# Two attention layers on one core: every engine's order from a list scheduler in the source, norms on ScalarE, layer 1's norm from layer 0's statistics

## Chip, cores, metric

One NeuronCore of a Trainium2 chip. The metric is device time in microseconds (us) of one execution.

## The reference, cut to what matters

Input x is 128 batches of 128 x 512 in float32, with a 128 x 128 adjacency mask for each batch. Two layers follow each other:

```python
x = layernorm(x + L0(x, adj))      # 4 heads of 64: q, k, v, masked softmax, out projection
x = layernorm(x + L1(x, adj))      # own norm first, then 8 heads of 64, mask | identity
# layernorm(x) = (x - mean) / sqrt(var + 1e-5); L1 norms its input again, with gamma and beta
```

So x1 = norm(y) leaves layer 0, and layer 1 first computes h = norm(x1). With v the variance of y, the mean of x1 is 0 and its variance is v / (v + eps). Hence h = (y - mean) / sqrt(v (1 + eps) + eps^2): both norms follow from one set of statistics of y.

## The kernel before

It works on groups of four batches (32 groups). A *unit* is eight heads' worth of attention: two batches of layer 0 or one of layer 1, so a group has 2 + 4 units. TensorE's order is written by hand; the other engines' order is the framework's. A slot starts one unit, finishes the unit two slots older, and puts *filling* (projections of other groups) between the stages in fixed shares:

```python
def slot(u, fill):
    stages = ((scores, u, 0.4), (attend, recent[1], 0.2), (residual, recent[1], 0.2),
              (probs_t, recent[0], 0.2))
    ...
        stage(unit)
        for step in fill[done:upto]:   # the share of filling after this stage
            step()
...
def residual(u):                       # the output projection, the sum and the norms
        nc.gpsimd.tensor_tensor(xb, xin, (bias0, bias1)[l], op=ALU.add)
        for c in range(nk):
            nc.tensor.matmul(pm, aT[:, j * nk + c, :], WO[l][:, c, :], ...)
        nc.vector.tensor_add(y, pm, xb)
        if l == 0:
            normed(X1[g][:, b, :], y, ...)
            normed(H[g][:, b, :], X1[g][:, b, :], ...)   # a second pass of statistics
        else:
            normed(y, y, ...)
...
def normed(dst, src, name):
    norm_stats(src, 0, mv)             # VectorE bn_stats, bn_aggr
    r = rstd_of(mv, 1)                 # GpSimd add eps, pow -0.5
    nc.vector.tensor_scalar(dst, src, mv[:, 0, 0:1], r, op0=ALU.subtract, op1=ALU.mult)
```

`attend` ends in an eviction from PSUM to the tile aT, and `residual` needs aT; only a fifth of the slot's filling lies between them. `probs_t` transposes the probabilities and evicts them to the tile pT. The eviction to aT is always ScalarE's; the others alternate between ScalarE and VectorE by the parity of an index.

Of the kernel before, what the change touches and what calls it, by code (L numbers as in the profile page):

```python
# [10 lines left out]
F32 = mybir.dt.float32  # L11
# [5 lines left out]
PE = mybir.EngineType.PE  # L17

P = 128
D = 64  # L20
# [4 lines left out]
SCALE = D ** -0.5  # L25


@with_exitstack
def kernel(ctx: ExitStack, tc: tile.TileContext, x, adj, wq, wk, wv, wo, bo,
# [9 lines left out]
    const = ctx.enter_context(tc.tile_pool(name="const", bufs=1))  # L39
    one = ctx.enter_context(tc.tile_pool(name="one", bufs=1))  # L40
    two = ctx.enter_context(tc.tile_pool(name="two", bufs=2))
    three = ctx.enter_context(tc.tile_pool(name="three", bufs=3))
    ps_sc = ctx.enter_context(tc.tile_pool(name="ps_sc", bufs=1, space=PSUM))
    ps_tr = ctx.enter_context(tc.tile_pool(name="ps_tr", bufs=2, space=PSUM))
    ps_ao = ctx.enter_context(tc.tile_pool(name="ps_ao", bufs=2, space=PSUM))
    ps_mm = ctx.enter_context(tc.tile_pool(name="ps_mm", bufs=2, space=PSUM))
    ctx.enter_context(tc.manual_schedule(engines={PE}))

    def tr_tile(name):
        return ps_tr.tile([P, 512], F32, tag="tr", name=name)  # L50

    def mm_tile(name):
        return ps_mm.tile([P, 512], F32, tag="mm", name=name)


    X, M = {}, {}

    def load(g):
        X[g] = two.tile([P, G, E], F32, tag="x", name=f"x_{g}")
        M[g] = three.tile([P, G, N], U8, tag="m", name=f"m_{g}")  # L60
        nc.sync.dma_start(X[g], x[g * G:(g + 1) * G].rearrange("b n e -> n b e"))
        nc.sync.dma_start(M[g], adj[g * G:(g + 1) * G].rearrange("b i j -> i b j"))

    load(0)


    ident = const.tile([P, P], F32, name="ident")
    make_identity(nc, ident)
    eye = const.tile([P, P], U8, name="eye")
    nc.vector.tensor_copy(eye, ident)  # L70
    mhalf = const.tile([P, G], F32, name="mhalf")
    nc.gpsimd.memset(mhalf, -0.5)

    w0 = const.tile([P, KC, 3 * INNER[0]], F32, name="w0")
    for i, w in enumerate((wq, wk, wv)):
        nc.sync.dma_start(w0[:, :, i * INNER[0]:(i + 1) * INNER[0]],
                          w.rearrange("(c p) f -> p c f", p=P))
    nc.gpsimd.tensor_scalar_mul(w0[:, :, :INNER[0]], w0[:, :, :INNER[0]], SCALE)
    wo0 = const.tile([P, INNER[0] // P, E], F32, name="wo0")
    nc.sync.dma_start(wo0, wo.rearrange("(c p) f -> p c f", p=P))  # L80
    bias0 = const.tile([P, E], F32, name="bias0")
    nc.sync.dma_start(bias0, bo[None, :].to_broadcast([P, E]))
    bias1 = const.tile([P, E], F32, name="bias1")
    nc.sync.dma_start(bias1, b_out[None, :].to_broadcast([P, E]))

    w1 = const.tile([P, KC, 3 * INNER[1]], F32, name="w1")
    wo1 = const.tile([P, INNER[1] // P, E], F32, name="wo1")
    gb_raw = const.tile([2 * KC, P], F32, name="gb_raw")
    gb = const.tile([P, 2 * KC], F32, name="gb")

    def transposed_weight(dst, src, name, r, scale):
        rows, cols = src.shape
        raw = two.tile([P, cols], F32, tag="raw", name=f"{name}_{r}")
        nc.sync.dma_start(raw, src[r * P:(r + 1) * P, :])

        def run():
            pt = tr_tile(f"{name}t_{r}")
            for c in range(cols // P):
                nc.tensor.transpose(pt[:, c * P:(c + 1) * P], raw[:, c * P:(c + 1) * P], ident)
            dst_r = dst[:, :, r * P:(r + 1) * P]  # L100
            src_r = pt.rearrange("p (c f) -> p c f", f=P)
            if r % 2:
                nc.vector.tensor_scalar_mul(dst_r, src_r, scale)
            else:
                nc.scalar.activation(dst_r, src_r, AF.Copy, scale=scale)
        return run

    def setup_layer1():

        nc.sync.dma_start(gb_raw[:KC], gamma.rearrange("(c p) -> c p", p=P))  # L110
        nc.sync.dma_start(gb_raw[KC:], beta.rearrange("(c p) -> c p", p=P))

        def gb_step():
            pt = tr_tile("gb_t")
            nc.tensor.transpose(pt[:, :2 * KC], gb_raw, ident[:2 * KC, :2 * KC])
            nc.vector.tensor_copy(gb, pt[:, :2 * KC])

        def step(dst, src, name, r, scale):
            def run():
                transposed_weight(dst, src, name, r, scale)()  # L120
            return run

        nq = INNER[1] // P
        return ([gb_step] + [step(w1, w_qkv, "w_qkv", r, SCALE if r < nq else 1.0) for r in range(3 * nq)]
                + [step(wo1, w_out, "w_out", r, 1.0) for r in range(E // P)])

    W = (w0, w1)
    WO = (wo0, wo1)
    X1, H, XT, QK, V = {}, {}, {}, {}, {}


    def transposed_steps(l, g):
        def chunk(c):
            def run():
                src = X[g] if l == 0 else H[g]
                if c == 0:
                    XT[l, g] = one.tile([P, KC, T], F32, tag=f"xT{l}", name=f"xT{l}_{g}")
                xT = XT[l, g]
                pt = tr_tile(f"xt{l}_{g}_{c}")
                for b in range(G):  # L140
                    nc.tensor.transpose(pt[:, b * N:(b + 1) * N], src[:, b, c * P:(c + 1) * P], ident)  # L141
                if l == 0:
                    if c % 2:
                        nc.vector.tensor_copy(xT[:, c, :], pt)
                    else:
                        nc.scalar.copy(xT[:, c, :], pt)
                else:
                    nc.scalar.activation(xT[:, c, :], pt, AF.Identity,
                                         bias=gb[:, KC + c:KC + c + 1], scale=gb[:, c:c + 1])
            return run  # L150
        return [chunk(c) for c in range(KC)]

    def project_steps(l, g):
        I = INNER[l]
        nq = I // P
        per = 512 // I
        steps = []
        box = {}

        def begin():  # L160
            QK[l, g] = one.tile([P, 2 * nq, T], F32, tag=f"qk{l}", name=f"qk{l}_{g}")
            V[l, g] = one.tile([P, G, I], F32, tag=f"v{l}", name=f"v{l}_{g}")

        def qk_step(f, c):
            def run():
                if f == 0 and c == 0:
                    begin()
                if c == 0:
                    box["pm"] = mm_tile(f"qk{l}_{g}_{f}")
                pm = box["pm"]  # L170
                nc.tensor.matmul(pm, W[l][:, c, f * P:(f + 1) * P], XT[l, g][:, c, :],  # L171
                                 start=(c == 0), stop=(c == KC - 1))
                if c == KC - 1:
                    if f % 2:
                        nc.scalar.copy(QK[l, g][:, f, :], pm)  # L175
                    else:
                        nc.vector.tensor_copy(QK[l, g][:, f, :], pm)  # L177
            return run

        def v_step(b0, b, cs):  # L180
            def run():
                if b == b0 and cs[0] == 0:
                    box["pm"] = mm_tile(f"v{l}_{g}_{b0}")
                pm = box["pm"]
                for c in cs:
                    nc.tensor.matmul(pm[:, (b - b0) * I:(b - b0 + 1) * I],  # L186
                                     XT[l, g][:, c, b * N:(b + 1) * N], W[l][:, c, 2 * I:3 * I],
                                     start=(c == 0), stop=(c == KC - 1))
                if b == b0 + per - 1 and cs[-1] == KC - 1:
                    src = pm.rearrange("p (b i) -> p b i", i=I)  # L190
                    if (b0 // per) % 2:
                        nc.scalar.copy(V[l, g][:, b0:b0 + per, :], src)
                    else:
                        nc.vector.tensor_copy(V[l, g][:, b0:b0 + per, :], src)
            return run

        for f in range(2 * nq):
            steps += [qk_step(f, c) for c in range(KC)]
        for b0 in range(0, G, per):
            for b in range(b0, b0 + per):  # L200
                steps += [v_step(b0, b, range(c, c + per)) for c in range(0, KC, per)]
        return steps



    SM, PT, AT = {}, {}, {}

    def batches(u):
        l, g, k = u
        per = 8 // HEADS[l]  # L210
        return range(k * per, (k + 1) * per)

# [206 lines left out]
```

## Time and profile before

| | before |
|---|---|
| median time | 4197.6 us |
| TensorE busy / idle | 3705 / 492 us |
| mean granted TensorE clock | 0.932 |
| VectorE, ScalarE, GpSimd busy | 1700, 1124, 1208 us |

"Busy" of TensorE counts pipelined matmuls at whatever clock they ran, so 88% busy does not mean 88% useful; the sum of the same work at full clock, 3320 us, is worked out in the prediction from the rows of a stretch without waits. The prediction also shows the lines of this profile. In them PE and PEld are TensorE's matmuls and its weight loads, DVE is VectorE, ACT ScalarE, POOL GpSimd and SP the engine that issues the transfers; a line of waits, "A <- B: 266.8, 128, 5.4", says that A waited for B 266.8 us in total, 128 times, at most 5.4 us.

### The profile page before, as it was taken

To read this page: it belongs to the slowest core of one execution; us is meant where nothing else is said; L and a number is where in the kernel's file an instruction comes from. 1 tells how busy PE (TensorE), PEld (TensorE's weight loads), DVE (VectorE), ACT (ScalarE), POOL (GpSimd) and SP (SyncE) were. 2 spreads that over 40 slices of the span, in tenths; PEclk is the share of its full clock that TensorE was granted. 3 is DMA by queue.
4 is the path that set the end of the run, shared out by engine and by line. 5 is a ranking of instruction groups with operands and counts; after the bars stand their busy time and mean duration, and the time that the engine had idled before them with its cause. 6 is when DMAs were issued, how large, how long until landed. Compare 5 with 4: busy or idle time off the path is not lost.

```text
span 4197.0 us, 41535 instructions
## 1 busy us (share of the span) xinstructions
PE 3705.4 (88%) x15425; PEld 1974.2 (47%) x15425; DVE 1700.0 (41%) x3242; ACT 1123.6 (27%) x3945; POOL 1208.2 (29%) x1608
## 2 busy tenths in 40 slices
PE   7999888998888988899888999888998888988888
PEld 4444444444444544444444444444444444544444
DVE  3433444334444334443344433444334444334433
ACT  2222222222222222222222222222222222222222
POOL 2222333222332223322233322332223332223332
PEclk8999999999999999999999999999999999999989
DMA  3000000000000000000000000000000000000000
GB/s 97 14 19 11 19 19 19 19 11 19 19 19 19 18 11 20 20 16 21 11 19 19 16 21 11 19 19 19 19 11 19 19 19 19 12 17 19 8 8 21
DMA packets 56890, 78.69 MB, mean 19 GB/s; under 512 B 19816, under 2 KB 21360, under 8 KB 56688
## 3 DMA queue, kind: packets, MB, share of 16 engines
q1 hardware_dynamic: 56688, 76.04, 5.4%
q8 instruction: 121, 1.98, 0.2%
q14 instruction: 81, 0.66, 0.1%
HBM read 42.47 MB, written 33.55 MB: 18 GB/s over the span
## 4 chain that ended last, share of the span: by engine, by line
PE 64%; DVE 13%; ACT 11%; POOL 9%; issue 3%; DMA 0%; ACTq 0%; POOLq 0%; DVEq 0%
PE qk L171 23%; PE o L313 18%; PE v L186 12%; ACT sm L245 9%; PE sc L234 4%; POOL rstd L291 4%; POOL xb L310 3%; PE pt L259 2%; DVE sm L239 2%; PE xt L141 2%; DVE st L283 2%; DVE nmax L243 2%; DVE x L298 2%; PE av L275 2%; DVE h L298 2%
## 5 line engine op out<-in xcount | busy, mean ns | idle before, releaser
L171 PE MATMUL qk<-xT,w 128*128 128x512 f32 x3072 | 1466.1, 615 | 0.0
L313 PE MATMUL o<-wo,aT 128*128 128x512 f32 x1536 | 835.0, 694 | 266.8 <-ACT aT L278 266.8
L171 PEld LDWEIGHTS qk<-xT,w 128*128 128x128 f32 x3072 | 567.3, 196 | 587.5 <-issue 571.5
L248 POOL TENSOR_TENSOR sm<-sm,rec 128x512 f32<-128x512 f32 x384 | 396.5, 1039 | 1282.5 <-DVE rec L247 1282.0
L245 ACT ACTIVATE sm<-sm,nmax 128x128 f32<-128x128 f32 x1536 | 593.7, 388 | 539.9 <-DVE nmax L243 539.8
L186 PE MATMUL v<-w,xT 128*128 128x256 f32 (+1 forms) x2048 | 729.5, 492 | 0.0
L310 POOL TENSOR_TENSOR xb<-x,bias 128x512 f32<-128x512 f32 x256 | 331.3, 1294 | 1286.4 <-DVE y L316 1277.0
L313 PEld LDWEIGHTS o<-wo,aT 128*128 128x128 f32 x1536 | 329.4, 222 | 731.8 <-issue 388.0
L316 DVE TENSOR_TENSOR y<-o,xb 128x512 f32<-128x512 f32 x256 | 176.9, 691 | 911.4 <-PE o L313 908.9
L186 PEld LDWEIGHTS v<-w,xT 128*128 128x128 f32 x2048 | 372.7, 190 | 267.8 <-issue 247.0
L239 DVE COPY_PREDICATED sm<-m,sc 128x512 f32<-128x512 uint8 x384 | 260.2, 714 | 142.2 <-PE sc L234 138.6
L261 ACT COPY pT<-pt 128x512 f32<-128x512 f32 x192 | 112.3, 585 | 748.2 <-PE pt L259 748.2
L245 ACT ACTIVATION_READ_ACCUMULATOR sm<-sm,nmax 128x1 f32 x1536 | 287.7, 187 | 0.0
L177 DVE COPY qk<-qk 128x512 f32<-128x512 f32 x192 | 132.5, 690 | 379.7 <-PE qk L171 379.7
L275 PEld LDWEIGHTS av<-pT,v 128*64 128x64 f32 x3072 | 183.9, 149 | 149.7 <-issue 144.5
L234 PE MATMUL sc<-qk 64*128 64x128 f32 x3072 | 252.0, 310 | 1.5 <-DVE sm L239 1.5
L141 PE MATMUL xt<-ident,h 128*128 128x128 f32 x512 | 97.7, 307 | 175.5 <-DVE h L298 111.2
L175 ACT COPY qk<-qk 128x512 f32<-128x512 f32 x192 | 111.8, 582 | 525.2 <-PE qk L171 525.2
L234 PEld LDWEIGHTS sc<-qk 64*128 64x128 f32 x3072 | 212.0, 210 | 80.3 <-issue 34.3
L243 DVE TENSOR_REDUCE nmax<-sm 128x4 f32<-128x512 f32 x384 | 245.5, 674 | 1.0
L275 PE MATMUL av<-pT,v 128*64 128x128 f32 x3072 | 230.9, 297 | 4.2 <-DVE pT L263 4.2
L223 POOL MEMSET sm<- 128x1024 f32 x192 | 182.7, 952 | 172.1 <-PE pt L259 170.9
(45 smaller groups left out, 2222.5 us busy)
## 6 DMA issues: line engine op xcount, KB each, us to landing
x<-in_x_dram SPq DMA_DIRECT2D x32, 1024.0 KB, 5.4
out_dram<-y SPq DMA_DIRECT2D x128, 256.0 KB, 2.0
w_qkv<-in_L_gnn_w_qkv_dram SPq DMA_DIRECT2D x12, 256.0 KB, 2.7
m<-in_adj_dram SPq DMA_DIRECT2D x32, 64.0 KB, 2.0
w_out<-in_L_gnn_w_out_dram SPq DMA_DIRECT2D x4, 256.0 KB, 2.6
w<-in_L_gnn_Wq_dram SPq DMA_DIRECT2D x1, 512.0 KB
w<-in_L_gnn_Wk_dram SPq DMA_DIRECT2D x1, 512.0 KB
w<-in_L_gnn_Wv_dram SPq DMA_DIRECT2D x1, 512.0 KB, 8.5
```

The lines of the kernel that those rows point to most:

```text
L141: nc.tensor.transpose(pt[:, b * N:(b + 1) * N], src[:, b, c * P:(c + 1) * P], ident)
L171: nc.tensor.matmul(pm, W[l][:, c, f * P:(f + 1) * P], XT[l, g][:, c, :], start=(c == 0), stop=(c == KC - 1))
L186: nc.tensor.matmul(pm[:, (b - b0) * I:(b - b0 + 1) * I], XT[l, g][:, c, b * N:(b + 1) * N], W[l][:, c, 2 * I:3 * I], start=(c == 0), stop= ...
L223: nc.gpsimd.memset(sm, (NEG0, NEG1)[l])
L234: nc.tensor.matmul(ps[:, s, i, :], qk[r, hp, t], qk[r, H2 + hp, t], start=True, stop=True)
L239: nc.vector.copy_predicated(sm[:, s].rearrange("p (b h) n -> p b h n", h=H2), mask[:, :, None, :].to_broadcast([P, len(bs), H2, N]), ps[:, ...
L243: nc.vector.tensor_reduce(nmax[:, s], sm[:, s], AX.X, ALU.max, negate=True)
L245: nc.scalar.activation(sm[:, s, i, :], sm[:, s, i, :], AF.Exp, bias=nmax[:, s, i:i + 1], accum_out=total[:, s, i:i + 1])
L248: nc.gpsimd.tensor_tensor(sm[:, s], sm[:, s], rec[:, s, :, None].to_broadcast([P, 4, N]), op=ALU.mult)
L275: nc.tensor.matmul(pa[s * D:(s + 1) * D, i, :], V[l, g][:, b, h * D:(h + 1) * D], pT[:, s, i, :], start=True, stop=True)
L310: nc.gpsimd.tensor_tensor(xb, xin, (bias0, bias1)[l], op=ALU.add)
L313: nc.tensor.matmul(pm, aT[:, j * nk + c, :], WO[l][:, c, :], start=(c == 0), stop=(c == nk - 1))
```

## The change

Intent: let every engine's order follow from priorities, data dependences, buffers and durations, so that independent projections fill each wait of the attention chain; and shorten the norms. The sources declare operations with their reads, writes and cost on each engine that may run them; a list scheduler picks, whenever an engine is free, the ready operation of lowest rank whose buffers are free; the instructions are then emitted in that order and the framework no longer reorders anything.

```diff
+class Plan:
+    HOP = 60.0
+    def op(self, rank, choices, emit, reads=(), writes=(), after=()): ...   # dependences, buffers
+    def run(self, engines):
+        ...            # whenever an engine is free: lowest (rank, seq) whose buffers are free
+                heapq.heappush(finished, (now + until + self.HOP, o.seq, o))
+MM = 429.0
+TR = 109.0
+DRAIN = 200.0
+ACTCOPY, DVECOPY = (493.0, 585.0), (605.0, 692.0)      # (engine free again, result there), ns
-    ctx.enter_context(tc.manual_schedule(engines={PE}))
+    ctx.enter_context(tc.manual_schedule())
+    p_xb = pool("xb", 3, [P, E])                          # fixed buffers; 2 before
+    p_sc = pool("sc", 2, [P, 512], F32, psum)             # was one buffer of two banks
+    FILL, TRANS, EVAC = 1e6, 1e5, -1.0                    # attention's rank is its unit's number
+    EITHER = {"ACT": ACTCOPY, "DVE": DVECOPY}             # evictions: whichever is free
...                                                       # (projections, one bank of four matmuls)
+        for f in range(2 * nq):
+            ps = Buf(p_mm)
+            for c in range(KC):
+                op(rank, PEQ(2 * MM), mm, reads=[(xT, c)] + wr[f // nq], writes=[(ps, 0)])
+            op(EVAC, EITHER, ev, reads=[(ps, 0)], writes=[(qk, f)])
...                                                       # (norm)
+            nc.gpsimd.tensor_scalar_add(at(8), at(7), EPS)
+            if l == 0:
+                nc.gpsimd.tensor_scalar(at(9), at(7), 1.0 + EPS, EPS * EPS, op0=ALU.mult, op1=ALU.add)
...                                                       # pow -0.5 on both, then -mean * rstd
+            nc.scalar.activation(dst, y.tile(), AF.Identity, bias=at(12 + a), scale=at(10 + a))
...
+    setup()
+    load(0)
+    order = plan.run(("PE", "DVE", "ACT", "POOL", "SP"))
+    for o in order:
+        o.emit(o)
```

## The prediction

> **What bounds the kernel now.** I read the page first, then the chain of work that ended last over one group of four batches, then the table of waits, the table by windows and the timeline of TensorE.
>
> ```profile
> span 4197.0 us, 41535 instructions
> PE 3705.4 (88%) x15425; PEld 1974.2 (47%) x15425; DVE 1700.0 (41%) x3242; ACT 1123.6 (27%) x3945; POOL 1208.2 (29%) x1608
> PEclk8999999999999999999999999999999999999989
> PE 64%; DVE 13%; ACT 11%; POOL 9%; issue 3%; DMA 0%; ACTq 0%; POOLq 0%; DVEq 0%
> ```
>
> TensorE is the busiest engine, but the chain of the end lies on it for only 64%; 33% is on the three elementwise engines. So TensorE stands idle while a softmax or a norm finishes. Its granted clock is also below full in every slice. The table by windows (columns: length, busy us of PE, PEld, DVE, ACT, POOL, granted clock, DMA share, GB/s) shows both halves of that:
>
> ```profile
> 2044.00:2100.00 56.00, 56.00 (x196) 27.36 (x195) 15.78 (x29) 12.81 (x43) 10.02 (x12) 0.99 0.03 10
> 2031.00:2044.00 13.00, 10.20 (x40) 6.34 (x42) 3.30 (x5) 2.55 (x5) 3.73 (x5) 0.79 0.05 20
> ```
>
> In one group of about 131 us there is a stretch of 56 us, packed with independent projection matmuls, where TensorE never stops, and a stretch where it waits. The chain of work in the packed stretch gives the unhindered cost of every kind of TensorE work (columns: start, us, what):
>
> ```profile
> 2063.28 4.29 PE qk L171 x10
> 2067.57 0.87 PE pt L259 x8
> ...
> 2072.32 1.09 PE sc L234 x16
> ...
> 2082.19 1.02 PE av L275 x16
> ```
>
> So 429 ns for a 512-wide matmul, 109 ns for a transpose, 1.09 us for the scores of a unit and 1.02 us for its attention product. Multiplied by the counts of the groups by line: qk 3072 x 0.429 = 1318 us; o 1536 x 0.429 = 659; v 1024 x 0.429 + 1024 x 0.215 (half the width) = 659; scores 192 x 1.09 = 209; attention product 192 x 1.02 = 196; transposes of probabilities 1536 x 0.109 = 167; of x and h 1024 x 0.109 = 112. The sum is **3320 us**, or 103.7 us for each of the 32 groups. No order of the same matmuls is shorter. The other 877 us are 492 us of idle TensorE (4197 - 3705) and 385 us in which it is busy but slow or draining. Where it idles and runs slow:
>
> ```profile
> PE o L313 <- ACT aT L278: 266.8, 128, 5.4
> ...
> PE xt L141 <- DVE h L298: 111.2, 34, 6.8
> ...
> PE xt L141 <- DVE pT L263: 64.2, 30, 2.1
> ```
>
> ```profile
> 2016.70 3.70 PE L313 MATMUL o<-wo,aT 128*128 128x512 f32 x8 [0.50 <-ACT aT L278]
> ...
> 2031.66 5.40 PE L313 MATMUL o<-wo,aT 128*128 128x512 f32 x8 [1.97 <-ACT aT L278]
> ```
>
> The output projection stands directly behind the attention product in the fixed order and waits for its eviction; the transposes of h wait for two norms in a row. The same eight matmuls take 3.70 us after a short wait and 5.40 us after a long one.
>
> **What the Trainium skill says.** (1) "TensorE: Matmul & The Clock Gate", Part 1: the array's clock is halved after an idle window of about 3.4 us and needs about as long a busy window to come back. The trace agrees in kind: clock 0.79 in the waiting window, 0.99 in the packed one, and 5.40 against 3.70 us. So closing the idle gaps also buys back clock. (2) "ScalarE: Activation LUTs", What ACT_TABLE_LOAD costs: an ACTIVATE with a pointer bias takes about 280 ns + 0.833 ns per element and 93 ns more for a second pointer, which is 0.80 us at 512 elements; the existing two-pointer row (xT<-xt,gb) shows 772 ns. The new norm on ScalarE has this form. All its functions already run behind one table load in the trace. (3) "SBUF — State Buffer", Who interferes with whom: a VectorE tensor_scalar in a two-port mode and a GpSimd instruction exclude each other. The trace agrees: tensor_scalar has a median of 546 ns and a maximum of 1487, and its means are 698 to 847. The change deletes all 384 of these.
>
> **The change part by part.**
>
> *The norms.* Removed from VectorE: 384 tensor_scalar (108.4 + 100.6 + 89.3 = 298 us), and the second pass of statistics of layer 0 (128 bn_stats, 88.5 us, and 128 bn_aggr, 21.8). Added on ScalarE: 384 applies at about 0.77 us = 296 us. GpSimd loses 128 separate pow calls (74 us) and gains small multiplies (256 at 0.22 = 56 us). These engines stand at 27 to 41%, so the sums alone give nothing. What counts is latency: from y to h was 691 + 178 + 220 + 579 + 546 for x1 and then as much again, some 4.5 us without waits; in the trace one such chain runs from 2003.03 to 2011.28, 8.3 us. After: 0.69 + 0.18 + about 0.4 + 0.65 + 0.2 on GpSimd + 0.75 on ScalarE = about 2.9 us. That brings layer 1's projection forward.
>
> *The order.* It is the main part. Each engine's program becomes the order of a list scheduler: attention first by unit number, then transposes, then projection matmuls as filling, evictions ahead of all, on ScalarE or VectorE, whichever is free. Its durations (429, 109, 1150 ns and so on) agree with the rows above or are slightly long, so the planned order should be executable as planned. Is there filling when attention waits? Worked by hand for a group: layer 1 attention needs 4 x (1.1 + 0.9 + 1.0 + 3.4) = 26 us of TensorE, layer 0 attention 2 x (1.1 + 0.9 + 1.0 + 3.4) = 13, transposes of x and h 3.5, and the projections, which have nothing to wait for but an eviction, 41.2 + 20.6 = 62. The latency of one unit is about 1.3 scores + 1.4 mask and max + 1.75 exp + 1.3 reciprocal and multiply + 1.2 transposes and eviction + 1.9 product and eviction + 3.4 output projection = 12 us, plus 3 for its norm; two units overlapped make about 25 us for layer 0, and in that time layer 0's projection of the next group (20.6 us) and layer 1's attention of the last group (26 us) are open. So filling exceeds the latency nearly everywhere.
>
> *Load on the others after*, per group: ScalarE 12 half units of exp at 1.54 us (eight exps of a unit took 3.08 us in the timeline) + 12 norms + 4 transposes' evictions at 0.77 = 31 us; VectorE 12 x (0.71 + 0.67 + 0.18) + 8 x (0.69 + 0.69 + 0.18) + 4 x 0.28 = 32; 40 free evictions at about 0.63 = 25 us between them. That is 44 us each of 104: no new bound. GpSimd: 6 x 0.95 + 12 x 1.04 + 8 x 1.29 + about 9 of small ones = 37 us.
>
> *Buffers.* The scores' two banks are freed one by one instead of together, xb gets a third buffer; the single qk, v, xT and h buffers stay, so a projection's eviction still waits for the scores of the group before. PSUM stays at four pairs of banks. These give little by themselves.
>
> *The sum.* 3320 of work + 64 weight transposes (7 us) + about 12 us at the start (TensorE began at 6.8 us; x is now issued behind the three weight loads) + about 20 us at the end, where the last four units have no filling (from 4150 on, before has 47 us for 26 us of work) + a leak of 3 us per group, which I choose for moments when both projection banks or both transpose banks are taken and for small misfits between plan and chip: 32 x 3 = 96. Total 3455, rounded to **3460 us**, a gain of some 740 us (18%).
>
> **The rivals.**
>
> *A: the waits move.* A frozen order can misfit: one late softmax stops the in-order engine, and the single qk, v and h buffers or early grabbed xb buffers can leave both projection banks full with nothing to do. If that leaves 10 to 12 us of each group, the time is about 3700. For it: no engine can reorder around a late input. Against: the packed 56 us window shows that TensorE runs such a mix without a stop when inputs are there.
>
> *B: an elementwise engine becomes the bound in bunches.* Attention goes first, so exps, norms and evictions come close together, and an eviction behind four exps waits 1.5 us. ScalarE and VectorE would be full in the attention third of each group and TensorE idle there at half clock: 5 to 7 us per group, 3550 to 3600. Against: 44 us of 104 on each.
>
> *C: the plan comes true.* A leak of 1 us per group and a clock above 0.98: about 3390.
>
> *D: the order is not the limit and nothing much changes*, above 4115: it needs the fixed buffers to bring back as much waiting as is removed. I see no line for that.
>
> **Range and chances.** C gives the low end, 3390; B, with part of A, the high end, 3610. The most likely lies nearer C, as attention overlaps with 62 us of filling per group. Faster by over 2%: 0.96; within 2%: 0.03; slower: 0.01.
>
> **What would show it.** Right: TensorE busy at 96% or more of the span, granted clock at 0.98 or more, the wait of o for aT gone from 267 us to under 30, the wait of xt for h to under 20, PE's share of the chain above 85%, tensor_scalar of the norm gone, ScalarE's new norm at 0.75 to 0.80 us. Wrong: TensorE under 93% or clock under 0.96 would mean rival A or B, and the table of waits would say whether it waits for aT and pT (B) or for freed banks and qk buffers (A). The prediction falls if matmuls in packed stretches take more than 429 ns, since the sum of 3320 rests on that.

## The result and the profile after

The median is **3509.7 us** (3509.4 to 3510.1) against 4197.6; the ratio is 0.836 (95% interval 0.835 to 0.838). From the page of the changed kernel:

```profile
span 3507.6 us, 41380 instructions
PE 3461.5 (99%) x15425; PEld 1827.4 (52%) x15425; DVE 1530.1 (44%) x2939; ACT 1217.5 (35%) x3992; POOL 1204.3 (34%) x1736
...
PEclk9999999999999999999999999999999999999999
...
PE 98%; ACT 1%; DMA 1%; DVE 0%; issue 0%; SPq 0%; POOL 0%; POOLq 0%; DVEq 0%; ACTq 0%
```

The number of matmuls is the same. TensorE's idle time fell from 492 to 46 us, its busy time from 3705 to 3461: of the 689 us of the two spans, 446 are idle time and 244 are busy time of the same matmuls. The clock accounts for about all of the 244: summed from the trace's clock record, TensorE was busy for 498 us of the kernel before while the granted clock was at half, and the same work at full clock is estimated at half of that, 249 us less (mean clock 0.932 before, 0.999 after). The chain that ended last lies on TensorE for 98%.

The table of waits of the changed kernel (who waited for whom: us in total, times, longest) has these as the largest waits of TensorE's matmuls:

```profile
PE tr L287 <- DMA raw<-in_L_gnn_w_qkv_dram: 19.9, 3, 17.6
PE tr L307 <- ACT xT L317: 13.2, 31, 0.4
...
PE ao L450 <- DVE aT L223: 0.8, 1, 0.8
```

The 267 us of the output projection for aT have become 0.8, and the waits for h are gone. What is left is mainly one wait of 17.6 us for a transfer at the start. The timeline shows how the same stretch of work now lies (start, length, engine, operation):

```profile
2030.46 3.70 PE L450 MATMUL ao<-wo,aT 128*128 128x512 f32 x8
2034.09 1.09 PE L433 MATMUL ao<-pT,v 128*64 128x128 f32 x16
2035.12 1.09 PE L420 MATMUL tr<-ident,sm 128*128 128x128 f32 x8
2036.14 1.16 PE L383 MATMUL sc<-qk 64*128 64x128 f32 x16
2037.23 3.70 PE L450 MATMUL ao<-wo,aT 128*128 128x512 f32 x8
...
2069.01 30.12 PE L333 MATMUL mm<-xT,w 128*128 128x512 f32 x68
```

Between a unit's attention product (L433) and its output projection (L450) now stand transposes and scores of other units, 2.1 us of work, while the eviction takes 0.6 to 0.7. The same block of 68 projection matmuls recurs every 108.20 us (at 1960.81, 2069.01, 2177.21): that is the time of one group, against a sum of 103.75 us of work.

### The profile page after: what moved, and what is told of

Its sections match the earlier page's. It is cut to its first block, busy times and chain, and to the rows that moved or that the text cites. A ratio compares the mean times of both kernels' runs of the same rounds, so it can differ in the third digit from the quotient of the medians.

```text
span 3507.6 us, 41380 instructions
## 1 busy us (share of the span) xinstructions
PE 3461.5 (99%) x15425; PEld 1827.4 (52%) x15425; DVE 1530.1 (44%) x2939; ACT 1217.5 (35%) x3992; POOL 1204.3 (34%) x1736
## 4 chain that ended last, share of the span: by engine, by line
PE 98%; ACT 1%; DMA 1%; DVE 0%; issue 0%; SPq 0%; POOL 0%; POOLq 0%; DVEq 0%; ACTq 0%
PE mm L333 38%; PE mm L346 20%; PE ao L450 19%; PE sc L383 6%; PE ao L433 6%; PE tr L420 5%; PE tr L307 3%; ACT xT L317 1%; DMA raw<-in_L_gnn_w_qkv_dram 0%; ACT sm L403 0%; PE tr L287 0%; DMA x<-in_x_dram 0%; DMA raw<-in_L_gnn_w_out_dram 0%; DVE sm L391 0%; DVE xT L223 0%
## 5 line engine op out<-in xcount | busy, mean ns | idle before, releaser
L333 PE MATMUL mm<-xT,w 128*128 128x512 f32 x3072 | 1388.0, 598 | 0.0
L403 ACT ACTIVATE sm<-sm,small 128x128 f32<-128x128 f32 x1536 | 593.6, 389 | 1027.4 <-DVE small L398 1023.7
L333 PEld LDWEIGHTS mm<-xT,w 128*128 128x128 f32 x3072 | 542.0, 190 | 694.6 <-issue 485.8
L411 POOL TENSOR_TENSOR sm<-sm,small 128x512 f32<-128x512 f32 x384 | 399.0, 1040 | 1327.8 <-DVE small L407 1316.3
L346 PE MATMUL mm<-w,xT 128*128 128x256 f32 (+1 forms) x2048 | 720.5, 497 | 0.0
L450 PE MATMUL ao<-wo,aT 128*128 128x512 f32 x1536 | 697.0, 596 | 0.8 <-DVE aT L223 0.8
L223 DVE COPY qk<-mm 128x512 f32<-128x512 f32 x384 | 265.5, 691 | 965.2 <-PE mm L333 965.1
L346 PEld LDWEIGHTS mm<-w,xT 128*128 128x128 f32 x2048 | 367.8, 189 | 266.7 <-issue 146.2
L450 PEld LDWEIGHTS ao<-wo,aT 128*128 128x128 f32 x1536 | 281.8, 190 | 316.7 <-issue 300.6
L403 ACT ACTIVATION_READ_ACCUMULATOR sm<-sm,small 128x1 f32 x1536 | 288.8, 188 | 0.0
L433 PEld LDWEIGHTS ao<-pT,v 128*64 128x64 f32 x3072 | 163.8, 136 | 143.6 <-issue 116.5
L433 PE MATMUL ao<-pT,v 128*64 128x128 f32 x3072 | 209.9, 279 | 0.9 <-DVE v L223 0.9
```

Of the source, the lines that this page charges most:

```text
L223: nc.vector.tensor_copy(dst, src)
L333: nc.tensor.matmul(ps.tile(), W[l][:, c, f * P:(f + 1) * P], xT.tile()[:, c, :], start=(c == 0), stop=(c == KC - 1))
L346: nc.tensor.matmul(ps.tile()[:, (b - b0) * I:(b - b0 + 1) * I], xT.tile()[:, c, b * N:(b + 1) * N], W[l][:, c, 2 * I:3 * I], start=(c == 0 ...
L403: nc.scalar.activation(sm.tile()[:, s, i, :], sm.tile()[:, s, i, :], AF.Exp, bias=stat(4 * s + i, 1), accum_out=stat(8 + 4 * s + i, 1))
L411: lambda o, s=s: nc.gpsimd.tensor_tensor(sm.tile()[:, s], sm.tile()[:, s], stat(16 + 4 * s)[:, :, None].to_broadcast([P, 4, N]), op=ALU.mult),
L433: nc.tensor.matmul(pa.tile()[s * D:(s + 1) * D, i * N:(i + 1) * N], v.tile()[:, b, h * D:(h + 1) * D], pT.tile()[:, s, i, :], start=True, ...
```

## The experiments

All times are medians. Runs ran beside the kernel before, whose median in every set was 4198 to 4199 us. All outputs are right. "Changed kernel" is the 3509.7 us one.

### 1. Only the norm, in the old order

```diff
-                normed(X1[g][:, b, :], y, f"{l}_{g}_{b}")
-                normed(H[g][:, b, :], X1[g][:, b, :], f"h_{g}_{b}")
+                # one bn_stats/bn_aggr of y; pow on (var+eps) and (var(1+eps)+eps^2); -mean*rstd
+                nc.scalar.activation(H[g][:, b, :], y, AF.Identity, bias=sh[:, 1:2], scale=r[:, 1:2])
+                nc.scalar.activation(X1[g][:, b, :], y, AF.Identity, bias=sh[:, 0:1], scale=r[:, 0:1])
```

> The kernel before, its order untouched, with only the new norm (applied on ScalarE, layer 1's norm from the same statistics). Theory (the order is nearly all of the gain, the norm only shortens one chain): TensorE's wait of the transposes of h for h (111 us) mostly goes, the wait of o for aT (267 us) stays; 4197 falls to 4080 to 4150. Rival (the norm's latency is a large part): below 4000.

Measured: **3890.8 us** (ratio 0.927), 308 us less, more than twice what the theory allowed: the rival holds. Lines of the table of waits of this run:

```profile
PE o L313 <- ACT aT L278: 230.8, 128, 3.1
...
PE xt L141 <- DVE pT L263: 10.4, 30, 0.3
PE xt L141 <- ACT h L330: 6.8, 3, 3.6
```

As expected, the wait for h falls (111 to 7 us) and that for aT stays (267 to 231). But the wait of the same transposes for pT went too (64 to 10 us), although nothing of pT was changed: its eviction had stood behind norms in VectorE's queue (at 2041.07 in the trace before, behind a norm's tensor_scalar that waited 1.28 us for GpSimd and took 1.14), and VectorE lost 369 us of work (1700 to 1331). And the clock rose from 0.932 to 0.966: TensorE's busy time fell by 117 us beside the 191 us of idle time.

### 2. Two stages of the old order exchanged, with other shares of filling

```diff
-        stages = ((scores, u, 0.4), (attend, recent[1], 0.2), (residual, recent[1], 0.2),
-                  (probs_t, recent[0], 0.2))
+        stages = ((scores, u, 0.25), (attend, recent[1], 0.35), (probs_t, recent[0], 0.2),
+                  (residual, recent[1], 0.2))
```

> The kernel before with one edit: the transposes of the probabilities of the next unit stand between a unit's attention product and its output projection, and a larger share of the filling too. Theory (the wait of o for aT is a fault of that one place in the order): that wait falls from 267 us to under 80, TensorE's clock rises, and the time falls by 250 to 400 us, to 3800 to 3950. Rival (the wait only moves to the next consumer, a list scheduler is needed): above 4100.

Measured: **3843.7 us** (0.915), 355 us less, as the theory had it. The edit has two parts, which no run separates: the exchange, and filling of 0.35 in place of 0.2 behind the attention product. From its table of waits:

```profile
PE xt L141 <- DVE h L298: 240.9, 65, 7.1
...
PE o L313 <- ACT aT L278: 0.7, 1, 0.7
```

The wait for aT is gone to 0.7 us, but part of the gain was given back: the wait of the transposes for h doubled (111 to 241 us), probably because the output projection, which leads to h, now stands later. A wait removed by hand showed the next one.

### 3. The new order with the old norm

```diff
-            nc.scalar.activation(dst, y.tile(), AF.Identity, bias=at(12 + a), scale=at(10 + a))
+            nc.vector.tensor_scalar(dst, src, at(k), at(k + 3), op0=ALU.subtract, op1=ALU.mult)
+            # h from a second bn_stats/bn_aggr/pow of x1; planned anew; p_xb: 8 buffers, not 3
```

> The changed kernel with the old norm back (VectorE tensor_scalar, a second pass of statistics for layer 1), planned anew by the same scheduler; 8 xb buffers in place of 3, since with 3 the plan locks up. Theory (filling hides the longer chain): 3510 to 3560, within 1.5% of the changed kernel, VectorE up to about 1800 us busy. Rival (the shorter norm is needed for the order to work): above 3600.

Measured: **3532.6 us** (0.842), within the theory's range. From its page:

```profile
PE 3485.4 (99%) x15425; PEld 1829.3 (52%) x15425; DVE 1823.9 (52%) x3514; ACT 963.2 (27%) x3673; POOL 1195.6 (34%) x1608
```

xb is the buffer for the sum of x and bias. The run's control, the changed kernel with 8 xb buffers (run 11), takes 3508.6. So the norm that is worth 308 us in the old order is worth 24 us in the new one, although VectorE now does 1824 us of work instead of 1529: the filling hides the longer chain. Read the other way, this run is the change of order without the norm: it takes 665 of the 688 us by itself. (It has the new fixed buffers too. They were not run alone; run 11 shows only that an xb pool above 3 changes next to nothing.)

### 4. Only TensorE's order held fixed

```diff
-    ctx.enter_context(tc.manual_schedule())
+    ctx.enter_context(tc.manual_schedule(engines={PE}))
```

> The changed kernel, but only TensorE's order is held fixed; the other engines' instructions are left to the framework's own ordering, as in the kernel before. Theory (TensorE's order is what counts, the others have slack at 35 to 44%): 3510 to 3580. Rival (the evictions and softmax pieces must stand where the plan put them): above 3650, with TensorE waiting for evictions.

Measured: **3597.6 us** (0.857), between theory and rival: 88 us are due to the order of the other engines. From its table of waits:

```profile
PE ao L450 <- ACT aT L221: 47.2, 32, 2.4
PE tr L307 <- ACT xT L317: 25.4, 32, 1.1
```

The order of TensorE's 15425 matmuls in the trace is the same, yet the output projection waits for aT again. In the stretch below, the attention product ends at 2000.38, but on ScalarE the norm of x stands before the eviction to aT and waits 2.52 us for GpSimd:

```profile
2001.55 0.81 ACT L482 ACTIVATE x<-y,small 128x512 f32<-128x512 f32 x1 [2.52 <-POOL small L477]
2002.27 0.56 ACT L221 COPY aT<-ao 128x512 f32<-128x512 f32 x1
```

Where the framework put the ScalarE work, the eviction came later, and TensorE's output projection stood until 2002.89. The slack of engines that are busy for 35 to 44% is not enough by itself; an eviction must come in time each time.

### 5. Both hand edits together, no scheduler

This is the edit of run 1 and that of run 2.

> The kernel before with both edits of the first two runs together: new norm and the transposes of the probabilities between attention product and output projection; no scheduler. Alone they gave 308 us and 355 us. Theory (they remove different waits, h for the transposes and aT for the output projection): nearly additive, 3550 to 3620, and the scheduler itself is then worth only the remaining 50 to 100 us. Rival (both lead to the same remaining gaps): above 3700.

Measured: **3712.4 us** (0.884). Alone the edits gave 308 and 355 us, together 486: not additive, and the theory's 3550 to 3620 is missed. TensorE is idle for 198 us and its clock is 0.974. From its table of waits:

```profile
PE xt L141 <- ACT h L330: 86.5, 34, 2.6
PE o L313 <- ACT aT L278: 45.6, 32, 3.1
PE pt L259 <- DVE rec L247: 26.2, 30, 0.9
```

The remaining waits are many small ones, each 30 to 34 times, once a group. The whole change's 203 us beyond this (order, buffers and evictions on whichever engine is free) consist of 152 us of idle time and 52 us of busy time.

### 6. Accumulation chains in TensorE's own order

In the plan, a matmul that adds to a bank waits for the full end of the one before (200 ns of drain and 60 of hop). So the plan does one pair of bank A, then one of bank B, and so on; both banks fill up together, and both evictions fall due together. Lines of TensorE's weight loads in the changed kernel, from its timeline, with the idle time before each and its releaser in brackets:

```profile
2076.50 0.19 PEld L333 LDWEIGHTS mm<-xT,w 128*128 128x128 f32 x1 [0.24 <-issue]
2076.93 0.19 PEld L333 LDWEIGHTS mm<-xT,w 128*128 128x128 f32 x1 [0.24 <-issue]
2077.88 0.30 PEld L333 LDWEIGHTS mm<-xT,w 128*128 128x128 f32 x2 [0.76 <-DVE qk L223]
2078.73 0.30 PEld L333 LDWEIGHTS mm<-xT,w 128*128 128x128 f32 x2 [0.56 <-DVE qk L223]
```

Weight loads normally start every 0.43 us, one matmul ahead. At 2077.88 the load has to wait until the eviction has freed the bank (it ended at 2077.82, from the timeline of VectorE), cannot be done ahead, and some 0.1 us is lost (an estimate from two such places in 16 matmuls); from 2077.88 to the next such place at 2084.93, 16 matmuls take 7.05 us instead of 6.86.

```diff
-                op(rank, PEQ(2 * MM), mm, reads=[(xT, c)] + wr[f // nq], writes=[(ps, 0)])
+                last = op(rank, PEQ(2 * MM), mm, reads=[(xT, c)] + wr[f // nq], writes=[(ps, 0)],
+                          chain=last)      # ready when TensorE is done issuing the one before
-    p_xb = pool("xb", 3, [P, E])
+    p_xb = pool("xb", 8, [P, E])
```

> The changed kernel, except that in the plan the four matmul pairs that accumulate in one bank follow each other in TensorE's own order instead of each waiting for the full end of the one before (which makes the plan alternate between the two projection banks, so that both fall due for eviction together). 8 xb buffers in place of 3, since with 3 this plan locks up. Theory (TensorE loses about 0.1 us at each bank that is evicted just in time, some 410 times): the wait of its weight loads for the evictions of qk and v (278 us in total now) falls under 60 us and the time to 3460 to 3485. Rival (a wait costs its 0.1 us even when long satisfied): 3500 to 3520.

Measured: **3469.7 us** (0.8265, interval 0.8254 to 0.8277), 38.9 us below its control of run 11, as the theory had it. The largest waits of weight loads for an eviction in the projections of this run (its L345 is L333 above), and the same block of projections in the timeline:

```profile
PEld mm L345 <- DVE qk L235: 21.9, 29, 0.8
```

```profile
2040.45 29.54 PE L345 MATMUL mm<-xT,w 128*128 128x512 f32 x68
```

The 278 us of these waits fell to some 22 and the block of 68 matmuls from 30.12 to 29.54 us, 0.58 less. Where the bank is long free, the wait costs nothing: the rival falls. A group takes 106.82 us instead of 108.20.

### 7. Evictions to ScalarE first

```diff
-    order = plan.run(("PE", "DVE", "ACT", "POOL", "SP"))
+    order = plan.run(("PE", "ACT", "DVE", "POOL", "SP"))
```

> The changed kernel with one edit: where both are free, the plan gives an eviction to ScalarE (585 ns) instead of VectorE (692 ns); now 384 of 384 qk evictions are VectorE's. Theory (the banks are freed just in time): 107 ns earlier takes most of the stalls away, 3475 to 3495. Rival (the stall is not the eviction's length): 3505 to 3520.

Measured: **3514.4 us** (0.837): the theory's time is missed, and the rival's range holds it. TensorE's busy time did fall (3461 to 3444 us), but its idle time grew from 46 to 69 us. From its table of waits:

```profile
PE tr L420 <- ACT xT L221: 26.5, 31, 1.4
```

The busy time fits a shorter wait for banks; but with work moved to ScalarE, evictions of xT there came late. This edit changes the whole plan, so it isolates little, and does not decide between theory and rival.

### 8. The start

TensorE's first work in the changed kernel, from the timeline:

```profile
17.60 1.94 PE L287 MATMUL tr<-ident,raw 128*128 128x128 f32 x8 [17.60 <-DMA raw<-in_L_gnn_w_qkv_dram]
21.39 2.30 PE L287 MATMUL tr<-ident,raw 128*128 128x128 f32 x8 [1.84 <-DMA raw<-in_L_gnn_w_qkv_dram]
23.48 2.50 PE L307 MATMUL tr<-ident,x 128*128 128x128 f32 x12
```

The plan holds that a piece of layer 1's weights arrives 3 us after a free queue and x after 8, so it ordered the weights' transposes first; on the chip the queue issued that transfer only at 10.7 us.

```diff
-    setup()
-    load(0)
+    load(0)
+    setup()
-        op(EVAC, {"SP": (100.0, 3000.0)},
+        op(EVAC, {"SP": (100.0, 12000.0 if name == "w1" and r < 2 else 3000.0)},
```

> The changed kernel with x loaded before the weights, and the plan told that the first two pieces of layer 1's weights arrive after 12 us instead of 3. TensorE now begins at 17.6 us with weight transposes, in the kernel before at 6.8 us with those of x. Theory (the plan's DMA time is wrong, TensorE's fixed order waits for the wrong transfer): 10 to 16 us less, 3493 to 3500. Rival (the start is bound by the transfers in any order): within 4 us of 3510.

Measured: **3506.2 us** (0.835), 3.5 us less: the theory is missed, and the time lies just within the rival's 4 us. TensorE began at 6.75 us, and then the next transfer that the plan believed early stopped it:

```profile
18.82 0.24 PE L270 MATMUL tr<-ident,gb_raw 8*128 8x8 f32 x1 [6.34 <-DMA gb_raw<-in_L_gnn_beta_dram]
```

One transpose of 0.24 us for gamma and beta, which nobody needs yet, holds up the x transposes behind it. So the run does not show the rival's reason either, that the start is bound by the transfers in any order.

### 9 and 10. Do the measured durations matter?

Run 9 is the control (the sum of x and bias planned after the unit's attention product; without that the plan of run 10 locks up), run 10 gives the plan 700 ns for everything but transfers:

```diff
+        if "SP" not in choices:
+            choices = {e: (700.0, 800.0) for e in choices}
```

> Control for the next run: the changed kernel, with the sum of x and bias planned only after the unit's attention product (so that it cannot hold an xb buffer for a unit that is not yet near, which would lock up the plan of the next run). Expected 3505 to 3525, as the changed kernel.

> The control before, but the plan takes 700 ns for every operation of every engine instead of the measured durations (a softmax half takes 1540, an output projection of layer 1 3430, a transposes' group 436). Theory (priorities and buffers decide most, but evictions and transposes then stand in the wrong places of TensorE's fixed order): 3560 to 3750. Rival (the durations hardly matter): within 1% of the control.

Measured: the control **3505.1 us** (0.835), flat durations **3486.2 us** (0.830): *faster* by 19 us. The theory falls; the time lies within the rival's 1% of the control, though the gain is clear of the noise (intervals 0.829 to 0.832 and 0.834 to 0.836). So the measured durations are not what makes this order good. The gain has, by the trace, the cause of run 6: with the wrong durations the plan staggers the banks, and the waits of weight loads for evictions of qk in the projections nearly vanish. From the table of waits of run 10 (its L335 and L348 are L333 and L346):

```profile
PEld mm L335 <- DVE qk L225: 6.6, 10, 0.8
...
PEld mm L348 <- DVE qk L225: 1.5, 2, 0.8
```

In run 9 these two kinds of wait are 151.7 and 45.6 us. TensorE's busy time is 3415 us against 3453 in the control, while its idle time is larger (70 against 50 us), so good durations may save some idle time; the whole plan differs, and no run isolates this.

### 11. Control for the 8 xb buffers

> Control for the runs with 8 xb buffers (old norm in the new order, bank chains): the changed kernel with 8 xb buffers in place of 3 and nothing else. Expected within 5 us of the changed kernel's 3510.

Measured: **3508.6 us** (0.836), as expected.

### 12. All that helped

Runs 6 and 8 together, gamma and beta's transfer planned to land after 16 us, and the transposes' operation made to take its target buffer too, so that it does not hold a transpose bank that cannot be evicted:

```diff
-               reads=[(src, 0 if l == 0 else b) for b in range(G)] + [(CONST, "ident")],
+               reads=[(src, 0 if l == 0 else b) for b in range(G)] + [(CONST, "ident"), (xT, "slot")],
```

> All that helped together: bank chains; x loaded first and the late transfers of the start (first layer 1 weights, gamma and beta) planned late; and the transposes of x and h planned only when their target buffer is free, so that they do not hold a transpose bank. Theory: 3470 of the bank chains less 10 for the start, and the freed transpose banks close further gaps: 3400 to 3445. Rival (the banks were not what held it): 3455 to 3470.

Measured: **3436.6 us** (0.8186, interval 0.8175 to 0.8197), 73 us below the changed kernel and the fastest of all. A group takes 106.10 us. In the table by windows TensorE is busy without a gap (columns as in the prediction):

```profile
2000.00:2108.00 108.00, 108.00 (x485) 58.47 (x485) 46.84 (x89) 39.23 (x127) 37.40 (x54) 1.00 0.06 21
```

The parts of the 33 us between run 6 and this one were not separated further: the period accounts for 32 x 0.72 = 23, the rest lies at the start and the end.

## Why the prediction was right, point by point

**The time.** 3460 was forecast with a range of 3390 to 3610; 3509.7 came. The direction, the size (18% forecast, 16% measured) and the place were right.

**The floor of 3320 us.** It held as a bound: the best version reached 3436.6. The projections in the packed block need 29.54 / 68 = 434 ns each with their drain and one bank wait (run 6), against the 429 assumed. In the changed kernel itself they took 30.12 / 68 = 443, so the prediction's own sign that it falls, packed matmuls above 429 ns, did come; the 14 ns cost 1 us of a group, and run 6 shows that most of it was waiting for banks.

**Idle and clock together.** Right: waits for aT 267 to 0.8, for h 111 to none shown, clock 0.932 to 0.999. Of ScalarE's new norm, 0.75 to 0.80 us was forecast and 0.81 measured. Runs 1, 2 and 5 also show less idle time than before, a higher clock (0.966, 0.959, 0.974) and less busy time. But "the trace agrees in kind" hides a difference from the idle window of about 3.4 us that the prediction cites. The long wait that the prediction shows, before 2031.66, is one of 1.97 us, and behind it the clock column (last but two) is at half, until 2035.1:

```profile
2031.90:2035.00 3.10, 3.10 (x4) 1.17 (x4) 0.00 (x0) 0.00 (x0) 0.00 (x0) 0.50 0.00 0
```

In the clock record of that trace, 57 of 60 waits of 1.9 to 2.2 us were followed at once by a stretch at half clock, so here much less than 3.4 us was enough, and the measurement decides. Nor is it the sum of idle time that counts: run 4 idles for 115 us, mostly in two waits a group of about 0.8 and 1.5 us, and keeps a clock of 1.000. The length of the half clock does agree: 92 of the 129 stretches last 3.4 us.

**The mis-sized terms.** The leak per group was put at 3 us; it is 108.20 - 103.75 = 4.45, or 142 us instead of 96. Start, end and weights were put at 39 us; they are 3507.6 - 32 x 108.20 = 45. These two make up the 52 us between the forecast's sum, 3455, and the span. As for its cause, the prediction named full banks and small misfits. Run 6 settles 1.2 to 1.4 us of the 4.45 on the two projection banks falling due together. The rest may in part be the change between kinds of matmul: in run 6, four v matmuls between two units' scores take 1.91 us (from 2072.73 to 2074.64 in its timeline) instead of 4 x 0.429 = 1.72. That this is due to the change of kind was not isolated by a run. A leak of this size could be read from the trace before: of the prediction's "385 us in which it is busy but slow or draining", half clock explains about 249 (estimated above), and the other 136 us are about what remained as busy time above the sum of work, 3461 - 3320 = 141. The change removed the waits and the half clock, but not an amount of this size; that its causes are the same before and after is not shown. The start was mis-sized as well; the reason given was x behind the weight loads. Run 8 shows that this alone was not it; the fixed order waited for whichever transfer the plan thought early.

**The parts of the change.** The step "the order is the main part" is right in this sense: the order alone takes 665 of the 688 us (run 3) and the norm then adds 24. But the norm alone takes 308 (run 1). The two parts remove overlapping waits, so no fixed share belongs to either. The prediction had seen the chain from y to h (8.3 us), but not that the norms also delayed other evictions in VectorE's queue, which run 1 showed.

**"Its durations agree, so the planned order should be executable as planned."** As a reason for the gain this step fell: run 10 did better with durations that were plainly wrong. It fell also in one place literally: the transfers' times at the start were not those of the chip.

**Rival A** (a frozen order misfits and the waits move) is real but small in the changed kernel (46 us of idle time in all, 17.6 of them at the start); its mechanism shows where the order of one party was taken away (run 4, +88 us), where a transfer was late (run 8), and where the plan locks up because xb buffers are held by units that cannot run yet (runs 6 and 10 needed another rule). **Rival B** (an elementwise engine becomes the bound) was not seen: VectorE is at 44%, ScalarE at 35% of the span, and in the busiest stretch of a group that was looked at, from 1991 to 2005 us, at 10.43 and 9.45 of 14.00 us, while TensorE does not stop. **Rival C** (a leak of 1 us) was not reached even by run 12, at 106.10 - 103.75 = 2.35 us.

## What to carry to other kernels

When the busiest engine idles for small waits, look for independent work to put between a result and its consumer; one edit of the order of stages and their shares of filling gave half of this gain. Look at the length of each wait too: here waits of about 2 us also halved TensorE's clock, and shorter ones mostly did not. Closing one gap by hand opened another (run 2), and two hand edits together fell 203 us short of the whole change; the scheduler did as well with flat durations as with exact ones. Then check what the plan's model does at the edges: a dependence that is too strict (the accumulation chain) cost 39 us here, and a transfer thought too early left TensorE standing for 17.6 us at the start.

## What the Trainium skill lacked or had wrong

- "TensorE: Matmul & The Clock Gate", Part 1, says that TensorE's queue pulls weight loads ahead of matmuls in flight. It does not say what it costs when the load waits for a bank that is freed only just then: about 0.1 us for each such place (run 6: 278 us of such weight-load waits fell to some 22, and 38.9 us of time went with them), while a bank freed earlier costs nothing.
- No page gives a cost for changing between kinds of matmul. In run 6, four 512-wide matmuls between two batches of 64-row scores take 1.91 us instead of 1.72; the cause is not isolated.
- "ScalarE: Activation LUTs", What ACT_TABLE_LOAD costs, was close: an estimate from its formula gives 0.80 us for an ACTIVATE of 512 elements with two pointer operands; the new norms measure 0.808 to 0.811 us from SBUF, and the older eviction from PSUM 0.775.
- "SBUF — State Buffer", Who interferes with whom, agrees with the runs: GpSimd's sum of x and bias had a longest time of 1517 ns before, 1276 in run 1, which took the tensor_scalars of the norm out of the old order, and 1279 in the changed kernel; with the old norm back (run 3) it was 1554.
- What the runs show of the clock gate's idle window stands above, at "Idle and clock together": 1.97 us of waiting were enough for half clock.
